# A graph network with two expert layers on one core: the mask of layer 1's hidden values moved from TensorE to VectorE

## The chip, the cores and the metric

The kernel runs on one core of a Trainium2 chip. The metric is the device time of one execution in microseconds (us). A core has five engines that run side by side and wait for one another through semaphores: TensorE (PE in the profile, with its weight loads shown apart as PEld), VectorE (DVE), ScalarE (ACT), GpSimd (POOL) and SyncE (SP). Each engine takes its instructions in a fixed order, which is settled when the program is built.

## The reference

`x` has 6250 rows (nodes) of 256 numbers; a list of 100,000 edges has a source, a target and a weight for each. There are two layers, and each has two parts, each added to `x`:

- a graph part: rows of a normalized `x` are gathered by edge source, scaled by the edge's weight and summed into the edge's target row, with a 256 x 256 weight before or after;
- a feed-forward part with experts: 8 experts mixed by a softmax in layer 0; in layer 1, 32 experts of which each token uses one.

The last part, cut to what matters here:

```python
logits = xf @ router_w.T + router_b
idx = jnp.argmax(logits, axis=-1)                       # one of 32 experts for each token
h = jnp.einsum('nd,ndh->nh', xf, jnp.take(W1, idx, axis=0)) + jnp.take(b1, idx, axis=0)
h = jax.nn.relu(h)                                      # 64 hidden values of that expert
out = jnp.einsum('nh,nhd->nd', h, jnp.take(W2, idx, axis=0)) + jnp.take(b2, idx, axis=0)
x = x + jax.nn.relu(out)
```

## The kernel before, in words

Nodes lie in 49 tiles of 128. An early stage sorts the edges, layer 0 follows, and from about 1700 us on layer 1 runs to the end. Only layer 1 matters here.

**The experts of layer 1.** All 32 experts' hidden values are computed for every token, 32 x 64 = 2048 of them, in NC1 = 16 chunks of 128 (two experts a chunk), with the hidden values on the partitions and the tokens along the free dimension. The values of experts not chosen have to become 0, so that the second product, which sums over all 2048, leaves the chosen expert's alone. The tokens go in blocks: one of three tiles and 23 of two (384 and 256 tokens). For each block:

- `norm_a` and `norm_b` normalize the tiles (`stats`, `scaled_tile`) and turn them with TensorE (`transposed`) into `nT`.
- `begin1` computes the logits (`pl`, L1227), finds the largest on VectorE (L1232 to L1238), and makes a one-hot of the chosen expert four times side by side (`hots`, ScalarE, L1240), turned by TensorE (`pg`, L1243) and copied to `hotT` (ScalarE, L1245): partition q has a 1 for the tokens whose expert is q modulo 32. VectorE also writes `cold`, its complement (L1247).
- `hidden1` makes chunk c: two products of W1 with `nT` into a PSUM tile `ph` (L1254; each is float32 and shows as two matmul instructions), then a product of `sel` with `cold` added to it (L1257, bfloat16). `sel` holds -2^127 where a hidden row belongs to the expert of that partition, so every hidden value of an expert not chosen gets a huge negative number added, and the relu on ScalarE (`hm`, L1259) makes it 0. `sel` is made once by VectorE (L1296).
- `outs1` multiplies `hm` with W2 and adds into the PSUM tile `py` (L1270); for the first chunk also the zeroing product L1264 and the chosen expert's bias (L1268). `end1` adds the relu of `py` to X (L1277) and writes the rows out.

**The graph sums of layer 1** run between these products. Of 782 columns of 128 edges, 64 are summed early and 718 in this stage. `columns1` takes for each column: a gather of 128 rows of `h1` by an indirect DMA issued from GpSimd (L215, 23 buffers `g`), a copy scaled by the weights on ScalarE (L245) and what that copy's rounding left on VectorE (L246), both into `m` (12 buffers), a one-hot `s` of the targets on VectorE for three columns at a time (L236, 5 buffers), and one product `acc` on TensorE (L293). Every eight columns a half tile of sums is complete: copied and added (L266 to L278), and after two of them turned and multiplied by the layer's weight (`by_weight`, L223 to L229) into X. The next block can begin when its tiles are there.

**The order.** The loop over blocks and chunks is written out: `sums.upto(...)` takes as many columns as a plan has set for that point, `hidden1` for the next chunk goes ahead of `outs1` for this one, and `begin1` of the next block stands in the middle of the present one (`rest`). A scheduler then settles each engine's order. In steady state a block of two tiles has 16 chunks and 32 columns. `ph` shares three PSUM buffers with `by_weight`, and `hm` has four.

Of the kernel before, what the change touches and what calls it, by code (L numbers as in the profile page):

```python
# [8 lines left out]
F32 = mybir.dt.float32  # L9
F32R = mybir.dt.float32r  # L10
BF = mybir.dt.bfloat16
# [41 lines left out]
def gnn_ffn_kernel(ctx: ExitStack, tc: tile.TileContext, a, out):  # L53
# [72 lines left out]
    good1 = const.tile([P, 1], F32, name="good1")  # L126
    off = const.tile([P, 1], F32, name="off")

    which_x = const.tile([P, NX1], F32, name="which_x")
    nc.gpsimd.iota(which_x, pattern=[[1, NX1]], base=0, channel_multiplier=-1, allow_small_or_imprecise_dtypes=True)  # L130
    order = const.tile([P, NX1], F32, name="order")
    nc.gpsimd.iota(order, pattern=[[-1, NX1]], base=NX1, channel_multiplier=0, allow_small_or_imprecise_dtypes=True)
    edges_rec, edges_val = a["edges_rec"], a["edges_val"]
# [697 lines left out]
    with outs_ctx, tc.tile_pool(name="layer0", bufs=1) as wp, \  # L831
# [367 lines left out]
        for t in blocks1[0]:  # L1199
            sT = wp.tile([P, 2, P], F32, tag="hT0", name="sT", bufs=2)  # L1200
            firsts.append(by_weight(psum, first_sums[:, t, :], sT, t, ("agg", 2) if t else ("tr", 1)))
            next(firsts[-1])
        for part in firsts:
            next(part)
        sums.upto(cum[-1] + NE + 1)
        add_missing(hs, (3, 4))
    sorted_ctx.close()
# [2 lines left out]
    with tc.tile_pool(name="layer1", bufs=1, reuse_waits="tile") as wp, \  # L1210
            tc.tile_pool(name="psum_y1", bufs=1, space=bass.MemoryType.PSUM, reuse_waits="tile") as psum_y:

        sel_x = wp.tile([P, NX1, H1], BF, name="sel")
        sel = sel_x.rearrange("q (c s) i -> q c (s i)", s=2)
        nought = wp.tile([P, 2 * D], BF, name="nought")

        done = []

        def begin1(pool, tiles, *ready):

            n = len(tiles)
            nw = n * P
            nT = norm_b(pool, psum, tiles, *ready)
            pl = psum.tile([P, NB, NX1], F32, tag="tr", name="pl", bufs=1)
            for j in range(n):
                for k in range(2):
                    nc.tensor.matmul(pl[:, j, :], nT[:, k, j * P:(j + 1) * P], rw[:, k, :],  # L1227
                                     start=(k == 0), stop=(k == 1))
            hot = work.tile([P, NB, NX1], F32, tag="hot", name="hot")
            top = work.tile([P, NB], F32, tag="top", name="top")  # L1230
            g, m = hot[:, :n, :], top[:, :n]
            nc.vector.tensor_tensor(g, pl[:, :n, :], br1[:, None, :].to_broadcast([P, n, NX1]), OP.add)  # L1232
            nc.vector.tensor_reduce(m, g, AX.X, OP.max)
            nc.vector.tensor_tensor(g, g, m[:, :, None].to_broadcast([P, n, NX1]), OP.is_equal)

            nc.vector.tensor_tensor(g, g, order[:, None, :].to_broadcast([P, n, NX1]), OP.mult)
            nc.vector.tensor_reduce(m, g, AX.X, OP.max)
            nc.vector.tensor_tensor(g, g, m[:, :, None].to_broadcast([P, n, NX1]), OP.is_equal)  # L1238
            hots = work.tile([P, NB, P // NX1, NX1], F32, tag="hots", name="hots", bufs=1)
            nc.scalar.activation(hots[:, :n], g[:, :, None, :].to_broadcast([P, n, P // NX1, NX1]), AF.Copy)  # L1240
            pg = psum.tile([P, NB * P], F32, tag="tr", name="pg", bufs=1)
            for j in range(n):
                turned = nc.tensor.transpose(pg[:, j * P:(j + 1) * P], hots[:, j], ident)  # L1243
            hotT = pool.tile([P, NB * P], BF, tag="hotT", name="hotT", bufs=2)
            done[:] = [turned, nc.scalar.activation(hotT[:, :nw], pg[:, :nw], AF.Copy)]  # L1245
            cold = pool.tile([P, NB * P], BF, tag="cold", name="cold", bufs=2)
            done.append(nc.vector.tensor_scalar(cold[:, :nw], pg[:, :nw], 0.5, None, op0=OP.is_lt))  # L1247
            return nT, hotT, cold, nw

        def hidden1(pool, block, c):  # L1250
            nT, _, cold, nw = block
            ph = psum.tile([P, NB * P], F32, tag="mm", name="ph", bufs=3)
            for k in range(2):
                nc.tensor.matmul(ph[:, :nw], w1f[:, k, c * P:(c + 1) * P], nT[:, k, :nw],  # L1254
                                 start=(k == 0), stop=False)

            nc.tensor.matmul(ph[:, :nw], sel[:, c, :], cold[:, :nw], start=False, stop=True)  # L1257
            hm = pool.tile([P, NB * P], F32, tag="hm", name="hm", bufs=4)
            nc.scalar.activation(hm[:, :nw], ph[:, :nw], AF.Relu, bias=b1[:, c:c + 1])  # L1259
            return hm  # L1260

        def outs1(block, c, now, py, n):
            for i in range(0, n, 2) if c == 0 else ():
                nc.tensor.matmul(py[:, i:i + 2, :], nought[:, :P], nought, start=True, stop=True)  # L1264
            for j in range(n):
                cols = slice(j * P, (j + 1) * P)
                if c == 0:
                    nc.tensor.matmul(py[:, j, :], block[1][:, cols], b2, start=False, stop=False,  # L1268
                                     skip_group_check=True)
                nc.tensor.matmul(py[:, j, :], now[:, cols], w2f[:, c, :], start=False, stop=(c == NC1 - 1),  # L1270
                                 skip_group_check=True)
# [12 lines left out]

        with tc.tile_pool(name="flow1", bufs=1, reuse_waits="tile") as flow:

            sums = Stream(columns1(flow, psum, range(NE, NREAL), h1, src_c, val_c, (5, EW + 6, 12, 4)))
            cum = [0] + [min(CS * (2 * tiles[-1] + 2) + CS // 2, NREAL) + LAG - NE for tiles in blocks1[1:]]
            rest = [(4, 2)] + [{2: (16, 6), 3: (12, 5), 4: (8, 3)}[len(tiles)] for tiles in blocks1[1:]]
            plans = aheads(cum, 2 * NC1, [r[0] for r in rest])  # L1290
            block = begin1(flow, *norm_a(blocks1[0]))

            behind = ExitStack()
            for ins in done:
                behind.enter_context(tc.issue_after(ins.ins))
            nc.vector.tensor_scalar(sel_x, which_x[:, :, None].to_broadcast([P, NX1, H1]), 0.0, FAR,  # L1296
                                    op0=OP.is_equal, op1=OP.mult)
            nc.vector.memset(nought, 0.0)
            hm = hidden1(flow, block, 0)
            for b, tiles in enumerate(blocks1):  # L1300
                n = len(tiles)
                last = b + 1 == len(blocks1)
                py = psum_y.tile([P, NB, D], F32, tag="y", name="py", bufs=1)
                mine = block
                for c in range(NC1):
                    sums.upto(plans[b][2 * c])
                    now = hm
                    if c + 1 < NC1:
                        hm = hidden1(flow, block, c + 1)
                    elif not last:  # L1310
                        block = after
                        hm = hidden1(flow, block, 0)
                    sums.upto(plans[b][2 * c + 1])
                    if b == 0 and c == 3:
                        behind.close()
                    outs1(mine, c, now, py, n)

                    if not last and c == NC1 - 1 - rest[b][0] // 2:
                        after = norm_a(blocks1[b + 1])
                    if not last and c == NC1 - 1 - rest[b][1]:  # L1320
                        after = begin1(flow, *after)
                end1(flow, tiles, py)

        with tc.tile_pool(name="slow1", bufs=1) as flow:

            def again():
                for t in range(NT):
                    block = begin1(flow, *norm_a([t]))
                    py = psum_y.tile([P, NB, D], F32, tag="y", name="py", bufs=1)
                    for c in range(NC1):  # L1330
                        outs1(block, c, hidden1(flow, block, c), py, 1)
                    end1(flow, [t], py)

            aggregate_any(psum, h1, True, again)
# [49 lines left out]
```

## Time and profile before

| | us |
|---|---|
| median of 3 runs | 2732.94 (2728.65 to 2740.33) |
| the profiled execution | 2729.55 |
| its span | 2727.7 |
| TensorE busy | 2589.7 (95%) |
| VectorE busy | 1993.3 (73%) |
| GpSimd busy | 1664.9 (61%) |
| ScalarE busy | 1652.4 (61%) |
| first and last gather of layer 1 start (718) | 1701.7 and 2637.5 |
| last output product ends, last output DMA issued | 2720.4, 2721.3 |

The span runs from the first to the last event of the profile. Busy times are unions of what the profiler recorded. The ends of matmuls are modelled, since they are pipelined: how long a matmul really occupies TensorE is read from the start of the next. A line such as `L246 DVE ... m<-g,val_c,m` names line, engine, operation, the tile written and the tiles read. In timelines the first column is the start, the second the duration, and the bracket at the end tells how long the engine had been idle and what ended it.

### The profile page before, as it was taken

The page shows a single profiled execution, that of the slowest core. Times are in us where ns is not written, and L with a number is a line of the kernel's source. Part 1 is how long each engine was busy: PE and PEld are TensorE (multiplying, and loading weights), DVE is VectorE, ACT ScalarE, POOL GpSimd, SP SyncE. Part 2 cuts the span into 40 slices and gives each one's busy share as a digit, 9 for nine tenths or more (in the row PEclk, how much of TensorE's full clock was granted, in tenths as well). Part 3 has the DMA queues.
Part 4 walks back from the last instruction along what each step waited for, and adds up shares of the span by engine and source line. Part 5 has one row for each costly group of instructions (what it writes and reads, how often), then busy time and mean ns, then how long its engine had stood idle before and what let it go on. Part 6 is the DMA issues. An engine that isn't in the chain of part 4 may idle for free.

```text
span 2727.7 us, 39992 instructions
## 1 busy us (share of the span) xinstructions
PE 2589.7 (95%) x11526; PEld 1880.3 (69%) x11527; DVE 1993.3 (73%) x5360; ACT 1652.4 (61%) x3915; POOL 1664.9 (61%) x1633
## 2 busy tenths in 40 slices
PE   5998788989899999999999999999999999999998
PEld 2666576867556666666666656678888888888887
DVE  8999887877687687787786657576666666666651
ACT  6999576655555555555555454466566666666652
POOL 0000757766776766766767445777777777777750
PEclk9999898999899999999999999999999999999999
DMA  6111433332332322332333233333333333333320
GB/s 203 55 47 55 152 109 113 106 111 82 102 94 86 106 90 81 107 88 83 105 90 93 70 93 110 95 111 105 110 111 106 110 110 106 111 109 106 111 79 10
DMA packets 132481, 267.36 MB, mean 98 GB/s; under 512 B 30564, under 2 KB 79800, under 8 KB 132248
## 3 DMA queue, kind: packets, MB, share of 16 engines
q0 software_dynamic: 77520, 211.78, 26.5%
q1 hardware_dynamic: 52568, 51.56, 5.9%
q8 instruction: 94, 1.54, 0.2%
q10 hardware_dynamic: 2160, 1.34, 0.2%
q14 instruction: 139, 1.14, 0.1%
HBM read 238.90 MB, written 25.67 MB: 97 GB/s over the span
## 4 chain that ended last, share of the span: by engine, by line
PE 74%; DVE 12%; DMA 5%; ACT 4%; issue 3%; POOL 1%; ACTq 0%; DVEq 0%; POOLq 0%; SPq 0%
PE ph L971 19%; PE ph L1254 12%; PE py L1270 12%; PE py L983 10%; PE acc L293 6%; PE acc L910 5%; DMA g<-h,idx 4%; PE put L614 2%; DVE m L246 2%; PE ph L1257 1%; PE ph L228 1%; DVE to L603 1%; PE ph L702 1%; ACT m L245 1%; POOL g L215 1%
## 5 line engine op out<-in xcount | busy, mean ns | idle before, releaser
L215 POOL DMA_INDIRECT g<-h,idx x822 | 860.4, 1047 | 386.8 <-DVE m L246 98.7
L215 POOL DMA_INDIRECT g<-h,src_c x718 | 715.6, 997 | 237.5 <-issue 94.5
L974 ACT ACTIVATE hT<-ph,shift,scale 128x512 f32<-128x512 f32 (+3 forms) x544 | 348.9, 654 | 298.4 <-PE ph L971 288.2
L245 ACT ACTIVATE m<-g,w 128x256 fp32r<-128x256 f32 x822 | 374.9, 500 | 217.5 <-PE acc L910 129.0
L246 DVE SCALAR_TENSOR_TENSOR m<-g,val_c,m 128x256 fp32r<-128x256 f32 x718 | 345.3, 483 | 205.0 <-ACT m L245 198.1
L245 ACT ACTIVATE m<-g,val_c 128x256 fp32r<-128x256 f32 x718 | 359.7, 504 | 125.6 <-PE acc L293 94.2
L1270 PE MATMUL py<-w,hm 128*128 128x256 f32 x1568 | 406.8, 379 | 1.3 <-ACT hm L1259 1.2
L1254 PE MATMUL ph<-nT,w 128*128 128x256 f32 (+1 forms) x1536 | 407.1, 385 | 0.0
L246 DVE SCALAR_TENSOR_TENSOR m<-g,w,m 128x256 fp32r<-128x256 f32 x822 | 370.3, 474 | 45.5 <-ACT m L245 44.4
L971 PE MATMUL ph<-nT,w 128*128 128x512 f32 (+3 forms) x1088 | 383.1, 482 | 19.2 <-ACT hT L974 18.9
L293 PE MATMUL acc<-m,s 128*128 128x512 f32 x782 | 398.9, 521 | 1.1 <-DVE m L246 1.0
L971 PE MATMUL ph<-hT,w 128*128 128x512 f32 (+3 forms) x1088 | 385.3, 481 | 6.5 <-ACT hT L974 6.4
L983 PE MATMUL py<-wo,hT 128*128 128x256 f32 x1568 | 383.1, 384 | 7.0 <-ACT hT L974 4.2
L910 PE MATMUL acc<-m,s 128*128 128x512 f32 x833 | 346.5, 501 | 17.2 <-DMA g<-h,idx 11.1
L983 PEld LDWEIGHTS py<-wo,hT 128*128 128x128 f32 x1568 | 291.8, 191 | 77.1 <-DVE X L985 18.0
L1259 ACT ACTIVATE hm<-ph,b 128x256 f32<-128x256 f32 (+1 forms) x384 | 183.4, 478 | 245.6 <-PE ph L1257 244.5
L1254 PEld LDWEIGHTS ph<-nT,w 128*128 128x128 f32 x1536 | 289.8, 191 | 47.3 <-issue 1.8
L1270 PEld LDWEIGHTS py<-w,hm 128*128 128x128 f32 x1568 | 287.1, 190 | 41.4 <-ACT hm L1259 2.4
L971 PEld LDWEIGHTS ph<-nT,w 128*128 128x128 f32 x1088 | 189.8, 193 | 145.8 <-issue 103.8
L971 PEld LDWEIGHTS ph<-hT,w 128*128 128x128 f32 x1088 | 194.6, 194 | 106.1 <-issue 74.0
L236 DVE TENSOR_TENSOR s<-col,dl 128x384 fp32r<-128x384 f32 (+1 forms) x294 | 155.7, 530 | 147.5 <-PE acc L910 147.1
L910 PEld LDWEIGHTS acc<-m,s 128*128 128x128 f32 x833 | 158.5, 193 | 102.8 <-DVE m L246 42.7
(301 smaller groups left out, 3175.2 us busy)
## 6 DMA issues: line engine op xcount, KB each, us to landing
g<-h,idx POOLq DMA_INDIRECT x822, 2.8
g<-h,src_c POOLq DMA_INDIRECT x718, 2.8
h<-hs SPq DMA_DIRECT2D x53, 128.0 KB, 1.7
own<-hs SPq DMA_DIRECT2D x49, 128.0 KB, 1.8
own<-own SPq DMA_DIRECT2D x49, 128.0 KB, 2.3
X<-in_x_dram SPq DMA_DIRECT2D x12, 512.0 KB, 8.3
out_dram<-o SPq DMA_DIRECT2D x22, 256.0 KB, 2.7
h<-hs SPq DMA_DIRECT2D x9, 512.0 KB, 3.1
```

Of the source, the lines that this page charges most:

```text
L215: nc.gpsimd.indirect_dma_start(out=g, out_offset=None, in_=h, in_offset=bass.IndirectOffsetOnAxis(ap=idx, axis=0))
L236: nc.vector.tensor_tensor(s[:, :n], col[:, None, :].to_broadcast([P, n, P]), dl[:, j:j + n, None].to_broadcast([P, n, P]), OP.is_equal)
L245: nc.scalar.activation(m[:, 0, :], g, AF.Copy, scale=w)
L246: newest[:] = [nc.vector.scalar_tensor_tensor(m[:, 1, :], g, w, m[:, 0, :], op0=OP.mult, op1=OP.subtract)]
L293: nc.tensor.matmul(acc, s[:, (j - js.start) % SJ, :], m, start=opens, stop=done)
L910: summed = nc.tensor.matmul(acc, s[:, j % SJ, :], m, start=(j == 0), stop=(j == EW - 1))
L971: nc.tensor.matmul(ph[:, :nw], (w1, w2)[layer][:, e, k, m * P:(m + 1) * P], src[:, k, :nw], start=(k == 0), stop=(k == 1))
L974: nc.scalar.activation(hT[:, m, :nw], ph[:, :nw], AF.Relu, bias=shift[:, layer, c:c + 1], scale=scale[:, layer, c:c + 1])
L983: nc.tensor.matmul(py, hT[:, k, j * P:(j + 1) * P], wo[:, e, k, :], start=(k == 0), stop=(k == 1))
L1254: nc.tensor.matmul(ph[:, :nw], w1f[:, k, c * P:(c + 1) * P], nT[:, k, :nw], start=(k == 0), stop=False)
L1259: nc.scalar.activation(hm[:, :nw], ph[:, :nw], AF.Relu, bias=b1[:, c:c + 1])
L1270: nc.tensor.matmul(py[:, j, :], now[:, cols], w2f[:, c, :], start=False, stop=(c == NC1 - 1), skip_group_check=True)
```

## The change

The mask goes from TensorE to VectorE. `sel`, `cold` and the product L1257 go. In their place:

- `begin1` makes one more product on TensorE after `hotT`: `ids`, a matrix whose row q holds the number q in all columns for q < 32 and 0 below, times `hotT` gives the number of the chosen expert of each token, on all partitions. ScalarE copies it to `chosen` (bfloat16).
- `expert`, made once, holds for each hidden row and chunk the number of the expert it belongs to.
- `hidden1` applies the relu as before, and then VectorE multiplies `hm` in place by 1 where `chosen` equals the row's `expert`, and by 0 elsewhere. Both tensor inputs of this instruction are in SBUF.
- The loop keeps two chunks of `hidden1` ahead of `outs1` instead of one, and in the first block the next block's `norm_a` and `begin1` come one chunk earlier.

```diff
-    which_x = const.tile([P, NX1], F32, name="which_x")
-    nc.gpsimd.iota(which_x, pattern=[[1, NX1]], base=0, channel_multiplier=-1, allow_small_or_imprecise_dtypes=True)
+    which_x = const.tile([P, NC1], F32, name="which_x")
+    nc.gpsimd.iota(which_x, pattern=[[2, NC1]], base=0, channel_multiplier=0, allow_small_or_imprecise_dtypes=True)
...
-            cold = pool.tile([P, NB * P], BF, tag="cold", name="cold", bufs=2)
-            done.append(nc.vector.tensor_scalar(cold[:, :nw], pg[:, :nw], 0.5, None, op0=OP.is_lt))
-            return nT, hotT, cold, nw
+            pe = psum.tile([P, NB * P], F32, tag="tr", name="pe", bufs=1)
+            nc.tensor.matmul(pe[:, :nw], ids, hotT[:, :nw], start=True, stop=True)
+            chosen = pool.tile([P, NB * P], BF, tag="chosen", name="chosen", bufs=2)
+            nc.scalar.activation(chosen[:, :nw], pe[:, :nw], AF.Copy)
+            return nT, hotT, chosen, nw
...
                 nc.tensor.matmul(ph[:, :nw], w1f[:, k, c * P:(c + 1) * P], nT[:, k, :nw],
-                                 start=(k == 0), stop=False)
-
-            nc.tensor.matmul(ph[:, :nw], sel[:, c, :], cold[:, :nw], start=False, stop=True)
+                                 start=(k == 0), stop=(k == 1))
             hm = pool.tile([P, NB * P], F32, tag="hm", name="hm", bufs=4)
             nc.scalar.activation(hm[:, :nw], ph[:, :nw], AF.Relu, bias=b1[:, c:c + 1])
+            nc.vector.scalar_tensor_tensor(hm[:, :nw], chosen[:, :nw], expert[:, c:c + 1], hm[:, :nw],
+                                           op0=OP.is_equal, op1=OP.mult)
...
-            rest = [(4, 2)] + [{2: (16, 6), 3: (12, 5), 4: (8, 3)}[len(tiles)] for tiles in blocks1[1:]]
+            rest = [(6, 3)] + [{2: (16, 6), 3: (12, 5), 4: (8, 3)}[len(tiles)] for tiles in blocks1[1:]]
...
+            nc.vector.scalar_tensor_tensor(expert, part.to_broadcast([P, NC1]), float(H1), which_x,
+                                           op0=OP.is_ge, op1=OP.add)
+            nc.vector.scalar_tensor_tensor(ids, part.to_broadcast([P, P]), float(NX1), part.to_broadcast([P, P]),
+                                           op0=OP.is_lt, op1=OP.mult)
...
-            nc.vector.tensor_scalar(sel_x, which_x[:, :, None].to_broadcast([P, NX1, H1]), 0.0, FAR,
-                                    op0=OP.is_equal, op1=OP.mult)
             nc.vector.memset(nought, 0.0)
-            hm = hidden1(flow, block, 0)
+            hms = [hidden1(flow, block, c) for c in range(2)]
...
-                    now = hm
-                    if c + 1 < NC1:
-                        hm = hidden1(flow, block, c + 1)
+                    now = hms.pop(0)
+                    if c + 2 < NC1:
+                        hms.append(hidden1(flow, block, c + 2))
                     elif not last:
-                        block = after
-                        hm = hidden1(flow, block, 0)
+                        hms.append(hidden1(flow, after, c + 2 - NC1))
```

More of the change, by code (lines that the diff above doesn't have):

```diff
@@ L1202, in gnn_ffn_kernel @@
             next(firsts[-1])
-        for part in firsts:
-            next(part)
+        for rest in firsts:
+            next(rest)
         sums.upto(cum[-1] + NE + 1)
@@ L1211, in gnn_ffn_kernel @@
             tc.tile_pool(name="psum_y1", bufs=1, space=bass.MemoryType.PSUM, reuse_waits="tile") as psum_y:
-        sel_x = wp.tile([P, NX1, H1], BF, name="sel")
-        sel = sel_x.rearrange("q (c s) i -> q c (s i)", s=2)
+        expert = wp.tile([P, NC1], F32, name="expert")
+        ids = wp.tile([P, P], BF, name="ids")
         nought = wp.tile([P, 2 * D], BF, name="nought")
@@ L1245, in begin1 @@
             done[:] = [turned, nc.scalar.activation(hotT[:, :nw], pg[:, :nw], AF.Copy)]
-            cold = pool.tile([P, NB * P], BF, tag="cold", name="cold", bufs=2)
-            done.append(nc.vector.tensor_scalar(cold[:, :nw], pg[:, :nw], 0.5, None, op0=OP.is_lt))
-            return nT, hotT, cold, nw
+            pe = psum.tile([P, NB * P], F32, tag="tr", name="pe", bufs=1)
[3 more added lines that the diff above has]
+            return nT, hotT, chosen, nw
         def hidden1(pool, block, c):
-            nT, _, cold, nw = block
+            nT, _, chosen, nw = block
             ph = psum.tile([P, NB * P], F32, tag="mm", name="ph", bufs=3)
@@ L1322, in gnn_ffn_kernel @@
                 end1(flow, tiles, py)
+                block = after
         with tc.tile_pool(name="slow1", bufs=1) as flow:
```

## The prediction

> **What bounds the kernel now.** The change lies wholly in layer 1, which fills the span from about 1700 us to its end at 2727.7 us, so I read the profile for that stage alone, starting with the busy times by stretch (us of the stretch, then TensorE, weight loads, VectorE, ScalarE, GpSimd, the granted clock, DMA share, GB/s):
>
> ```profile
> core 0: us, PE busy (x) PEld busy (x) DVE busy (x) ACT busy (x) POOL busy (x), PEclk, DMA share, GB/s
> 1720.00:1900.00 180.00, 175.51 (x820) 137.12 (x820) 121.77 (x301) 104.68 (x244) 138.40 (x136) 0.99 0.36 105
> 1900.00:2600.00 700.00, 698.79 (x3455) 572.89 (x3454) 481.83 (x1175) 426.79 (x996) 535.49 (x541) 1.00 0.37 109
> ```
>
> TensorE is busy 699 of 700 us at full clock, which alone would make it the bound. GpSimd looks idle a quarter of the time, and that is the trap. The view of waits shows what its idle time consists of (total, times, longest):
>
> ```profile
> ACT m L245 <- PE acc L293: 94.2, 223, 1.6
> POOL g L215 <- issue: 88.6, 291, 0.3
> POOL g L215 <- DVE m L246: 57.3, 188, 0.3
> ACT m L245 <- DMA g<-h,src_c: 18.6, 28, 1.6
> ```
>
> Between 1720 and 2720 us no pause of the gather queue is longer than 0.3 us, whatever it is put down to. Its timeline has 0.30 us in front of every gather, and a gather that nothing disturbs lasts 0.946 (the median of 718). So GpSimd runs without a break from 1701.7 to 2637.5 us: 718 gathers, one each 1.30 us, and it cannot issue faster than one in 1.246. TensorE needs 41.43 us for a block of two tiles (from one `pl` in the chain of waits to the next, 2560.65 to 2602.08) and takes in 32 columns, one each 1.295 us. **Two engines are full at nearly the same rate.** From column 180 on ScalarE's m waits for TensorE's acc (94 us) rather than for gathers (18.6 us, all but 0.9 of it before 1900): TensorE is the bound there, with no room behind it.
>
> Why gathers take 1.30 and not 1.246 is seen in the timeline (start, duration):
>
> ```profile
> 2315.24 0.56 DVE L236 TENSOR_TENSOR s<-col,dl_c 128x384 fp32r<-128x384 f32 x1
> 2315.28 1.33 POOL L215 DMA_INDIRECT g<-h,src_c  x1 [0.30 <-DVE hot L1238]
> ...
> 2323.20 0.42 DVE L267 TENSOR_TENSOR sums<-sums,acc 128x256 f32<-128x256 f32 x1 [0.78 <-ACT sums L266]
> 2323.20 0.95 POOL L215 DMA_INDIRECT g<-h,src_c  x1 [0.30 <-issue]
> ```
>
> In the first pair both inputs of the VectorE instruction are in SBUF, and the gather lasts 0.38 us too long; in the second one input is in PSUM and the gather is undisturbed. It holds for the stage: of the 541 gathers from 1900 to 2600 us, those that find VectorE idle 0.1 us after their start last 0.003 us longer than 0.946 on average (179 of them), those that find L267 0.004 (31), those that find m of L246, with two SBUF inputs, 0.071 (163), and s of L236 0.133 (86). A held gather goes on when that VectorE instruction ends.
>
> **The change part by part.** The rows it touches, from the groups by shape between 1720 and 2720 us (busy us, mean ns):
>
> ```profile
> L246 DVE SCALAR_TENSOR_TENSOR m<-g,val_c,m 128x256 fp32r<-128x256 f32 x718 | 345.3, 483 | 205.0 <-ACT m L245 198.1
> L236 DVE TENSOR_TENSOR s<-col,dl_c 128x384 fp32r<-128x384 f32 x240 | 134.4, 560 | 18.3 <-PE acc L293 14.5
> L1257 PE MATMUL ph<-cold,sel 128*128 128x256 bf16 x368 | 100.2, 273 | 0.0
> L1247 DVE TENSOR_SCALAR cold<-pg 128x256 bf16<-128x256 f32 x23 | 9.6, 418 | 2.9 <-ACT hotT L1245 2.9
> ```
>
> Removed on TensorE: 384 mask products. Their 273 ns is a modelled end; what one occupies is read from starts, at the end of the kernel where no gathers are left:
>
> ```profile
> 2710.12 1.03 PE L1254 MATMUL ph<-nT,w 128*128 128x256 f32 x4
> 2710.98 0.27 PE L1257 MATMUL ph<-cold,sel 128*128 128x256 bf16 x1
> 2711.09 1.03 PE L1270 MATMUL py<-w,hm 128*128 128x256 f32 x4
> ```
>
> From 2710.98 to 2711.09 is 0.108 us (mean over neighbours). 368 of these and 16 half as long again are 42.3 us. Added on TensorE: 24 products with `ids`, 2.6 us. If TensorE alone decided, the gain would be 40 us. ScalarE gains 24 copies of 0.38 us, at 61% load and off the path. VectorE loses `sel` (1.2 us), 24 `cold` (10 us), and gains 384 multiplies. The multiply (two SBUF inputs, one bf16, 256 columns) does not occur before; the nearest row is L246, same operation and width: 0.483 us. A PSUM-reading twin, L1277, takes 0.42 and 0.56 is the 384-wide s: bounds 0.42 and 0.56, 345 of them (those of the chunks before 2637.5 us) 145 to 193 us; I take 167. VectorE, 69% busy now, comes to about 83% of a stage of similar length: full enough to be late, not the bound.
>
> The wait added is hm on VectorE: the multiply waits for ScalarE's relu, and behind it stand m and s of later columns. The look-ahead becomes two chunks, so between a chunk's ph and its py TensorE has five acc and two chunks' worth of other products, about 4.5 us, against 0.47 for the relu plus 0.48 for the multiply and some queueing: covered; uncovered it would cost what it is late, some 0.5 us a chunk. In `begin1` the product with `ids` follows `pg` after two ph and one acc (about 0.65 us) and waits for `hotT`, which is ready 0.55 us after `pg` at 2315.87: no more than a few tenths a block. No DMA and no other queue is moved.
>
> With the TensorE share of a block down to 41.43 - 16 x 0.108 + 0.11 = 39.8 us, 1.244 a column, **GpSimd is late next**: its floor is 1.246. From there only the holding counts. Call e the mean extra time of a gather: now 0.997 - 0.946 = 0.051. Instructions with two SBUF inputs (m, s and 38 us of half-tile sums) fill 517 us of the 923 in which columns are processed, 56%; with 167 more it is 71% of some 960 us. What e becomes is not in the trace, and bounds are far apart:
> - low: 0, as the gathers from 1711 to 1718 us, spaced 1.25 beside an idle VectorE, or 0.02 if they happen to fall between instructions;
> - in proportion, 0.051 x 71/56 = 0.065;
> - in proportion from the stretch in which TensorE waits for gathers, 1720 to 1900 us, whose gathers last 138.40/136 = 1.018, e 0.072: 0.091. There m runs as soon as its gather lands, and what is queued behind it runs just when the next gather starts;
> - high: at random moments, 71% x half of 0.483 = 0.17.
>
> I take 0.091, since the changed stage is of that kind throughout: gather-bound. The last gather then starts at 2637.5 + 717 x 0.040 = 2666 us. Behind it lie 90.2 us now. 39 mask products go (4.2 us). About 5 us more go because TensorE trails less: now column 700 is summed 18.7 us after its gather starts, while in the changed instruction order the multiply of a chunk stands behind an m only 7 columns ahead of the chunk's py, 7 x 1.3 plus the shortest 3.5 us from gather to m, some 13 us. 2666 + 81 = 2747, plus the 1.85 us by which the profiled execution (2729.55) exceeds its span: **2749 us**. Those runs' median is 2732.94, 3.4 above that execution, so this is +0.7% of the one and +0.6% of the other. In general the time is 2749 + 717 x (e - 0.091).
>
> The Trainium skill has a rule that speaks against this change: "SBUF — State Buffer", section "Who interferes with whom", says that a VectorE instruction with two SBUF inputs and a GpSimd instruction that reads SBUF exclude each other, the later one fully blocked until the first is done. The rows at 2315 and 2323 us agree, but the page gives no price; taken literally for gathers at random moments it is the high end, 2806, where the mean extra of the rows gives 2730 to 2749.
>
> **The rivals.**
> - *The holding grows only in proportion* (e 0.065): 2730. For it: the 0.071 per meeting with an m, which would add only about 0.012 for 17% more of such meetings. Against it: the gather-bound stretch. No change to be seen; 0.25.
> - *The gathers slip between the multiplies* (e about 0.02): one place, GpSimd's start of a gather. A gather held until an instruction's end is back at the same point 1.246 us later; queued instructions start 0.40 us apart (three m in 1.26 us at 1720.36), 0.45 to 0.5 behind an s, so m, multiply and s take about 1.3, and the hold repeats with only some 0.05 us, and with none where VectorE is between columns. Time 2698; faster as soon as e is under 0.045, the bound of 0.5%. TensorE's 39.8 us a block does not let it go far below 2684. Against it: three without an s take 1.20, and the gather then meets the next at its start. 0.20.
> - *The gathers meet VectorE at random* (e 0.14 to 0.17): 2784 to 2806, taken as 2795. For it: from 1718 to 1726 us, with VectorE's instructions back to back, gathers last 1.67, 1.07, 1.36, 1.35, 0.99. Against: 179 of 541 still find it idle. 0.18.
> - *VectorE itself becomes the bound*: needs a multiply over 0.48 + (960 - 800)/345 = 0.94 us; no row comes near. That the change does not do what it says is excluded by the instruction order: no sel product is left.
>
> **How the numbers follow.** Forecast 0.37, the others as given. The measurement tells about 0.5%, 14 us. Faster is the slipping case, 0.20; within 0.5% (2716 to 2743, e 0.045 to 0.083) is the proportional case, 0.25; slower the forecast and the random case, 0.55. The range leaves out half of the random case and the best of the slipping one: 2700 to 2795; around the forecast alone 2743 to 2775.
>
> **What would show it.** Right: gathers' mean duration rises from 0.997 to about 1.04 with pauses still 0.3, the last starts near 2666, TensorE shows idle time in front of acc or py, waits of ScalarE's m for gathers outweigh those for acc, and 0.108 us a chunk is saved after the last gather. Wrong: TensorE still without gaps and a block near 39.8 us (the holding did not grow), or a multiply far from 0.48 us, or VectorE without gaps.

## The result, and the profile after

The changed kernel takes 2748.31 us (median of 9 runs, 2742.48 to 2753.94), the kernel before on the same chip 2732.18 (9 runs, 2728.29 to 2740.33): ratio 1.0057, 95% interval 1.0041 to 1.0072, slower by some 16 us. The profiled execution took 2752.75 us, with a span of 2750.9. It lies 4.4 us above its kernel's median, and the profiled execution of the kernel before 2.6 below its own, so the two profiles differ by 23.2 us where the medians differ by 16.

Busy times by stretch, of the kernel after (us of the stretch, then TensorE, weight loads, VectorE, ScalarE, GpSimd, granted clock, DMA share, GB/s):

```profile
core 0: us, PE busy (x) PEld busy (x) DVE busy (x) ACT busy (x) POOL busy (x), PEclk, DMA share, GB/s
1720.00:1900.00 180.00, 168.69 (x733) 134.19 (x732) 137.03 (x338) 105.58 (x244) 139.12 (x135) 0.96 0.35 104
1900.00:2600.00 700.00, 668.98 (x3126) 558.60 (x3125) 544.75 (x1390) 417.30 (x988) 540.38 (x524) 0.98 0.36 105
```

TensorE is no longer full: 669 of 700 us, where it was 699. VectorE went from 482 to 545 us. GpSimd has as much busy time as before (540 against 535 us) but starts 524 gathers in it instead of 541: each is longer.

Seven rows of the waits of the kernel after between 1720 and 2740 us (total, times, longest):

```profile
ACT m L245 <- DMA g<-h,src_c: 159.3, 243, 2.1
DVE hm L1260 <- ACT hm L1259: 74.1, 116, 1.9
ACT m L245 <- PE acc L293: 66.5, 75, 3.3
POOL g L215 <- issue: 64.6, 212, 0.3
POOL g L215 <- DVE m L246: 51.8, 170, 0.3
PEld tr L356 <- ACT nT L357: 32.3, 21, 4.1
POOL g L215 <- DVE hm L1260: 31.4, 103, 0.3
```

Two rows have changed places: ScalarE's m now waits 159 us for gathers (18.6 before) and 67 us for acc (94 before). The gathers' own pauses are still 0.3 us at the longest: the queue is full as before, and now everything else waits for it.

Three groups of the page of the kernel after (busy us, mean ns of one, idle time before them):

```profile
L215 POOL DMA_INDIRECT g<-h,src_c x718 | 740.4, 1031 | 242.8 <-issue 66.7
L246 DVE SCALAR_TENSOR_TENSOR m<-g,val_c,m 128x256 fp32r<-128x256 f32 x718 | 343.3, 480 | 157.0 <-ACT m L245 152.5
L1260 DVE SCALAR_TENSOR_TENSOR hm<-chosen,expert,hm 128x256 f32<-128x256 bf16 (+1 forms) x384 | 186.6, 486 | 77.4 <-ACT hm L1259 75.3
```

The mean gather went from 0.997 to 1.031 us. One held gather in the timeline of the kernel after (start, duration):

```profile
2035.10 0.48 DVE L246 SCALAR_TENSOR_TENSOR m<-g,val_c,m 128x256 fp32r<-128x256 f32 x1
...
2035.27 1.60 POOL L215 DMA_INDIRECT g<-h,src_c  x1 [0.30 <-DVE hm L1260]
...
2035.50 0.55 DVE L236 TENSOR_TENSOR s<-col,dl_c 128x384 fp32r<-128x384 f32 x1
```

It meets an m, and an s directly behind it; it ends at 2036.87, 0.82 us after the s does (2036.05). So a hold can run on through a second instruction that follows without a gap. It does so seldom, and behind an m more often than elsewhere: of 77 gathers held over 0.05 us by an m with an s directly behind it, 19 were held to the end of the s; of 74 held by a multiply with an m behind it, 1 to the end of the m; of 59 held by an s with an m behind it, 1 (before, after and e7_idle_sbuf together, 1720 to 2630 us).

The whole difference of the two spans lies in three terms, read from the starts of the first and last gather. The last two columns are experiments told below:

| us | before | after | e7_idle_sbuf | e12_psum_pad |
|---|---|---|---|---|
| first gather starts | 1701.7 | 1708.9 | 1697.0 | 1701.8 |
| from it to the last one's start (717 intervals) | 935.8 | 958.0 | 961.1 | 943.8 |
| from there to the span's end | 90.2 | 84.0 | 88.9 | 83.5 |
| span | 2727.7 | 2750.9 | 2747.1 | 2729.1 |
| mean of 718 gathers | 0.997 | 1.031 | 1.036 | 1.006 |

The kernel after loses 7.2 us at the first gather and 22.2 in the gathers' pace, and gains 6.2 behind the last one: 23.2 us of span. Part of the first loss is made up at once, since the kernel before has one long pause in its queue, in front of the second gather; its line in the timeline of before:

```profile
1705.71 0.94 POOL L215 DMA_INDIRECT g<-h,src_c  x1 [3.08 <-issue]
```

e12_psum_pad has one there too (4.19 us), the kernel after and e7_idle_sbuf have none. Counted from the second gather on, the kernel after starts 4.5 us late (1710.2 against 1705.7), and its pace costs 24.9 us more (956.7 against 931.8).

The gathers between 1900 and 2600 us, sorted by what VectorE does 0.1 us after they start: how many, and by how much they exceed 0.946 us in sum.

| VectorE | before | after | e7_idle_sbuf | e12_psum_pad |
|---|---|---|---|---|
| idle | 179, 0.3 | 91, 0.2 | 107, 0.3 | 108, 0.1 |
| m (L246) | 163, 11.3 | 188, 22.6 | 141, 15.3 | 160, 15.2 |
| s (L236) | 86, 11.4 | 75, 12.7 | 73, 13.1 | 80, 12.9 |
| the multiply | none | 88, 6.6 | 100, 12.1 | 101, 0.2 |
| all | 541, 24.8 | 524, 45.5 | 525, 44.1 | 535, 31.9 |

In these four traces 701 gathers of this stretch last over 0.05 us longer than 0.946, and every one of them ends 0.81 to 0.83 us after the end of a VectorE instruction that reads only SBUF: m, s, the multiply from SBUF, a half-tile sum or another with two tiles there, and in 16 cases `xn` (L362), which reads one tile and two numbers per row. None ends so after an instruction with an input in PSUM.

### The profile page after: what moved, and what is told of

The parts are those of the page before. It is cut to its first block, busy times and chain, and to the rows that moved or that the text cites. A ratio compares the mean times of both kernels' runs of the same rounds, so it can differ in the third digit from the quotient of the medians.

```text
span 2750.9 us, 39554 instructions
## 1 busy us (share of the span) xinstructions
PE 2574.7 (94%) x11167; PEld 1886.4 (69%) x11167; DVE 2115.4 (77%) x5721; ACT 1658.5 (60%) x3939; POOL 1690.1 (61%) x1633
## 4 chain that ended last, share of the span: by engine, by line
PE 59%; DVE 15%; DMA 13%; ACT 5%; issue 5%; POOL 2%; ACTq 0%; DVEq 0%; POOLq 0%; SPq 0%
PE ph L971 19%; PE py L983 10%; DMA g<-h,src_c 8%; PE py L1272 7%; PE ph L1256 7%; PE acc L910 5%; DMA g<-h,idx 4%; PE acc L293 3%; DVE m L246 3%; ACT m L245 2%; PE put L614 2%; POOL g L215 2%; DVE to L603 1%; PE ph L702 1%; PE pl L1227 1%
## 5 line engine op out<-in xcount | busy, mean ns | idle before, releaser
L215 POOL DMA_INDIRECT g<-h,src_c x718 | 740.4, 1031 | 242.8 <-issue 66.7
L246 DVE SCALAR_TENSOR_TENSOR m<-g,val_c,m 128x256 fp32r<-128x256 f32 x718 | 343.3, 480 | 157.0 <-ACT m L245 152.5
L293 PE MATMUL acc<-m,s 128*128 128x512 f32 x782 | 440.4, 576 | 1.1 <-DVE m L246 1.0
L1256 PE MATMUL ph<-nT,w 128*128 128x256 f32 (+1 forms) x1536 | 416.6, 390 | 0.0
L1272 PE MATMUL py<-w,hm 128*128 128x256 f32 x1568 | 414.6, 386 | 0.0
L246 DVE SCALAR_TENSOR_TENSOR m<-g,w,m 128x256 fp32r<-128x256 f32 x822 | 370.1, 474 | 41.7 <-ACT m L245 40.3
L910 PE MATMUL acc<-m,s 128*128 128x512 f32 x833 | 346.5, 501 | 15.1 <-DMA rw<-in_router_t_dram 11.0
L236 DVE TENSOR_TENSOR s<-col,dl 128x384 fp32r<-128x384 f32 (+1 forms) x294 | 155.5, 529 | 150.3 <-PE acc L910 150.1
L1260 DVE SCALAR_TENSOR_TENSOR hm<-chosen,expert,hm 128x256 f32<-128x256 bf16 (+1 forms) x384 | 186.6, 486 | 77.4 <-ACT hm L1259 75.3
```

Source lines behind the costliest of these rows:

```text
L215: nc.gpsimd.indirect_dma_start(out=g, out_offset=None, in_=h, in_offset=bass.IndirectOffsetOnAxis(ap=idx, axis=0))
L246: newest[:] = [nc.vector.scalar_tensor_tensor(m[:, 1, :], g, w, m[:, 0, :], op0=OP.mult, op1=OP.subtract)]
L293: nc.tensor.matmul(acc, s[:, (j - js.start) % SJ, :], m, start=opens, stop=done)
L910: summed = nc.tensor.matmul(acc, s[:, j % SJ, :], m, start=(j == 0), stop=(j == EW - 1))
L1260: nc.vector.scalar_tensor_tensor(hm[:, :nw], chosen[:, :nw], expert[:, c:c + 1], hm[:, :nw], op0=OP.is_equal, op1=OP.mult)
```

## The experiments

My theory was that GpSimd's queue of gathers sets the time, that it can run no faster than one in 1.246 us, and that a VectorE instruction with two inputs in SBUF holds a gather, so that what TensorE saves counts for little and the multiply costs what it holds. The rivals: the time VectorE is busy, or the changed order, did it; or TensorE alone sets the time.

e1 to e6 and e8 to e11 ran on chips on which the kernel before itself takes 3162 to 3204 us, with pauses of several us on every engine from about 200 us on, so their times are compared only with the kernel before on the same chip, and the microseconds expected for them were not to be met there. Waits of e8_psum between 2000 and 2900 us show it (total, times, longest):

```profile
POOL g L215 <- DVE m L246: 135.8, 135, 4.0
ACT m L245 <- issue: 105.9, 68, 7.1
POOL g L215 <- issue: 105.9, 298, 1.9
```

The queue of gathers has pauses of up to 4 us there, and is not full. How long one gather lasts, and what holds it, can be read on these chips all the same. e7 and e12 ran on chips that are like that of the main result, with one execution each beside one of the kernel before.

**e7_idle_sbuf: the multiply alone, TensorE's work left as it was.** The kernel before, with one more instruction behind the relu:

```diff
             nc.scalar.activation(hm[:, :nw], ph[:, :nw], AF.Relu, bias=b1[:, c:c + 1])
+            spare = pool.tile([P, NB * P], F32, tag="spare", name="spare", bufs=2)
+            nc.vector.scalar_tensor_tensor(spare[:, :nw], cold[:, :nw], good1, hm[:, :nw],
+                                           op0=OP.is_equal, op1=OP.mult)
```

> The kernel before, mask product kept, with one more VectorE instruction per chunk in layer 1: the multiply of the change, on the chunk's relu output in SBUF, into a tile that nobody reads. TensorE's work and what is computed stay those of before. My theory (a VectorE instruction with two SBUF inputs that runs 0.1 us after a gather's start holds that gather): the mean gather rises from 0.997 us to 1.02 to 1.05, and where gathers follow one another after 0.30 us the time rises by 718 times that rise, 17 to 38 us, ratio 1.006 to 1.014. Rival (the loss came from the order of the work, the wait on the relu or the smaller tiles, not from the instruction itself): mean gather 0.99 to 1.00 and ratio 1.000 to 1.002.

Measured: 2748.97 us against 2733.10 of the kernel before, ratio 1.0058 (one run each, so no interval); the 15.9 us are just under the bound of 17. The first gather starts 4.7 us earlier than in the kernel before, which was not expected and whose cause was not tested; without it the bound would have been met. The mean gather is 1.036 us. Busy time of e7_idle_sbuf by stretch, columns as above:

```profile
1900.00:2600.00 700.00, 686.95 (x3351) 562.30 (x3351) 548.68 (x1400) 410.15 (x963) 540.06 (x526) 0.99 0.36 106
```

Nobody reads what this instruction writes, no order around it was changed, and the mask product is still there; yet the gathers slow down as in the changed kernel. By the table of terms, e7's pace is only 3.2 us slower than that of the kernel after, and its end only 4.9 us longer: **beside this multiply, TensorE's 40 us are worth about 8 us.** That is one execution of each kernel, and nine executions of the kernel after lie up to 11 us apart; it is far from 40 all the same. The rival of the order is not needed: the multiply alone slows the gathers as much. The timeline of e7_idle_sbuf shows the hold and its condition (two pairs, start and duration):

```profile
1975.97 0.48 DVE L1261 SCALAR_TENSOR_TENSOR spare<-cold,good,hm 128x256 f32<-128x256 bf16 x1
1976.12 1.15 POOL L215 DMA_INDIRECT g<-h,src_c  x1 [0.30 <-DVE m L246]
...
2100.44 0.94 POOL L215 DMA_INDIRECT g<-h,src_c  x1 [0.30 <-DVE st L345]
2100.45 0.45 DVE L1261 SCALAR_TENSOR_TENSOR spare<-cold,good,hm 128x256 f32<-128x256 bf16 x1
```

In the first pair the multiply starts 0.15 us ahead of the gather, which then ends 0.82 us after the multiply. In the second the gather starts first, by 0.01 us, and nothing happens to it.

**e12_psum_pad: the same multiply, its second input in PSUM.** The changed kernel; relu written back into PSUM, and an unused tile that puts the gather buffers where they lay before:

```diff
+        spare = wp.tile([P, NX1 * H1 - P - 2 * NC1], BF, name="spare")
...
+            nc.vector.memset(spare[:, :2], 0.0)
...
-            nc.scalar.activation(hm[:, :nw], ph[:, :nw], AF.Relu, bias=b1[:, c:c + 1])
-            nc.vector.scalar_tensor_tensor(hm[:, :nw], chosen[:, :nw], expert[:, c:c + 1], hm[:, :nw],
+            nc.scalar.activation(ph[:, :nw], ph[:, :nw], AF.Relu, bias=b1[:, c:c + 1])
+            nc.vector.scalar_tensor_tensor(hm[:, :nw], chosen[:, :nw], expert[:, c:c + 1], ph[:, :nw],
                                            op0=OP.is_equal, op1=OP.mult)
```

> The kernel of e6_psum_pad: relu written back into PSUM and read there by the multiply, and the gather buffers where they lay before. Where gathers follow one another after 0.30 us, as in e7_idle_sbuf, my theory gives a mean gather of 0.985 to 1.005, so 1.285 to 1.305 per gather; a first gather at 1698 to 1703; a last one 717 times that later, at 2619 to 2639; and a tail of 79 to 86 us: a span of 2700 to 2723 and a time of 2702 to 2725, under the kernel before because the products that are gone shorten the tail. Rival 1 (the multiply costs its time wherever its input lies): mean gather 1.03, time 2738 to 2748. Rival 2 (TensorE is the only full engine once the gathers are not held): 2690 to 2698. That the late first gather comes from the order of the work would show as a first gather near 1709.

Measured: 2730.91 us against 2738.25 of the kernel before (one run each). That is under all nine runs of the kernel after and within the nine of the kernel before (2728.29 to 2740.33): the loss is gone, a gain is not shown. Busy time by stretch, the multiply's group and a pair of the timeline of e12_psum_pad, a fence for each:

```profile
1900.00:2600.00 700.00, 677.69 (x3182) 568.95 (x3181) 554.40 (x1412) 422.13 (x1004) 537.01 (x536) 0.99 0.38 108
```

```profile
L1261 DVE SCALAR_TENSOR_TENSOR hm<-chosen,expert,ph 128x256 f32<-128x256 bf16 (+1 forms) x384 | 184.4, 481 | 72.3 <-ACT ph L1260 69.7
```

```profile
2000.98 0.47 DVE L1261 SCALAR_TENSOR_TENSOR hm<-chosen,expert,ph 128x256 f32<-128x256 bf16 x1
...
2001.12 0.94 POOL L215 DMA_INDIRECT g<-h,src_c  x1 [0.30 <-DVE s L236]
```

VectorE is busier than in the kernel after (554 us against 545), the multiplies are as many and take nearly the same time (481 ns against 486; those of 256 columns 475 against 481), yet a gather that starts 0.14 us behind one is not held. So it is not VectorE's busy time (rival 1: 2738 to 2748). Nor does the time fall to 2690 to 2698, as it should if TensorE alone set it (rival 2). My own 2702 to 2725 was missed by 6 us: first gather (1701.8) and end (83.5) came as expected, the pace did not (1.316 us an interval, against at most 1.305). Of the 8 us that this makes, 4 are the pause in front of the second gather. By the second table the multiply holds nothing any more (0.2 us), but m and s hold 5.4 us more in these 700 us than in the kernel before; why they meet more gathers is open.

All meetings with a multiply between 1900 and 2600 us (on the pausing chips 2000 to 2900), by how far ahead of the gather it starts:

| multiply reads | kernels | 0.08 to 0.30 us ahead | 0.03 ahead to 0.08 behind |
|---|---|---|---|
| two inputs in SBUF | after, e7 | 98 gathers, +0.167 us, 94 held | 60, +0.005, none held |
| one in SBUF, one in PSUM | e12 | 43, +0.001, none held | 37, +0.002, none held |
| one in SBUF, one in PSUM | e8, e10, e11 | 116, +0.001, none held | 113, +0.003, none held |

Held means over 0.05 us longer than 0.946. The Trainium skill, "SBUF — State Buffer", section "Who interferes with whom", states both halves: leaving aside what it calls the 2-port modes, a VectorE instruction with at most one SBUF input does not contend with GpSimd, and one with two SBUF inputs contends with a GpSimd instruction that reads SBUF. It adds that the order of issue decides who blocks. The runs agree where VectorE comes first, and add the price. That a gather which comes first blocks VectorE they do not show: in the kernel before, m takes 0.483 us when it begins 0.05 to 0.45 us into a gather (198 of them), and 0.483 us when it begins 0.45 to 0.9 us into one (193).

At the border the order alone does not settle it. In e3_pad and e4_kept, told below, whose multiply reads SBUF on a pausing chip, 8 of 78 gathers of the last column are held, by up to 1.2 us: in all eight the multiply starts 0.01 to 0.02 us ahead, directly behind an m that still runs.

**e1_psum, e8_psum: relu back into PSUM, nothing else.** The two changed lines of e12, without the unused tile, on two chips.

> Only the operand of the multiply changes: ScalarE writes the relu back into PSUM in place, and VectorE multiplies from there, so the multiply has one input in SBUF instead of two; same number of VectorE instructions, same waits. Theory (GpSimd's gathers set the pace, and VectorE instructions with two SBUF inputs hold them): the mean gather falls from 1.031 us to 0.99 to 1.00, the last gather starts near 2638 us, and the time is 2715 to 2730 us, faster than before by a little. Rival (VectorE's load, or the wait of the multiply for the relu, delays the chunks): gathers may change but the time stays at 2740 to 2750.

> The changed kernel with layer 1's relu written back into its PSUM tile and the multiply reading that tile from PSUM: one SBUF input (chosen) and one PSUM input instead of two in SBUF; the multiply's count and size as in the change. On this chip GpSimd is expected to keep its 0.30 us between gathers. My theory: the mean gather falls from 1.031 us to 0.985 to 1.005 and the last gather starts at 2632 to 2650 (first one still late, near 1709), so the time is 2713 to 2732, ratio to the kernel before 0.993 to 1.000. Rival 1 (any VectorE instruction holds a gather in proportion to VectorE's busy time): mean gather 1.03, time 2745 to 2752. Rival 2 (TensorE's order sets the time): TensorE's work is that of the change, so 2745 to 2752 too, with a mean gather anywhere.

Measured: ratios 0.9999 (0.9967 to 1.0031) and 0.9999 (0.9971 to 1.0027); mean gather 0.991 and 0.999 us. The gathers come as expected: they last as long as without any multiply (0.990 to 0.998, next paragraph), where the same multiply from SBUF makes it 1.023 and 1.034 (e3_pad, e4_kept). The small gain in time that was expected does not show; the times say nothing of a full queue there.

**e2_nomask, e5_nomask2, e9_nomask: no mask at all in layer 1**, one kernel on three chips:

```diff
-            nc.vector.scalar_tensor_tensor(hm[:, :nw], chosen[:, :nw], expert[:, c:c + 1], hm[:, :nw],
-                                           op0=OP.is_equal, op1=OP.mult)
```

> The multiply is left out, so the values of experts not chosen are not made 0; TensorE is without the mask product, all else as in the changed kernel. Theory (gathers set the pace once TensorE is relieved): the mean gather is 0.99 to 1.02 us and the time 2718 to 2735 us, though TensorE has 40 us less work than before. Rival (TensorE was the only bound before, and what was lost is VectorE's time): about 2692 us.

> The kernel without the multiply once more (the values of experts not chosen are not made 0), since on the chip of the first four runs every engine paused for 1 to 5 us at a time and the kernel before took 3196 us. On a chip without these pauses: theory (gathers set the pace once TensorE is relieved): mean gather 0.99 to 1.02 us, time 2718 to 2735 us. Rival (TensorE was the only bound before): about 2692 us.

> The changed kernel with the multiply left out as well, so that no mask is applied in layer 1 and the output is not the reference's: TensorE's 40 us are saved and VectorE's 177 us are not added. My theory (the gathers are a queue that is full): the mean gather is 0.985 to 1.005, the pauses stay 0.30 us, and 718 gathers from 1709 end near 2632 to 2645; with a tail of 79 to 84 us the time is 2711 to 2729, so most of TensorE's 40 us is still not seen. Rival (TensorE was the only full engine): the time falls by all of it, to 2690 to 2696.

Measured: ratios 0.9937 (0.9912 to 0.9963), 0.9938 (0.9909 to 0.9966) and 0.9968 (0.9944 to 0.9991), 10 to 20 us by the ratios and 15 to 27 by the medians; mean gather 0.990, 0.998, 0.992. Even with no multiply at all, TensorE's 40 us are not seen in full (at most 29 by the intervals). As the queue is not full on these chips, this does not show that the gathers are what keeps the rest.

**e3_pad: the change with the unused tile alone** (its two lines in the diff of e12).

> The changed kernel with an unused tile of the size by which its fixed tiles became smaller (3.8 KB a partition), so that the gather buffers lie where they lay before. If the place of the buffers made the first gather wait for ScalarE's last reading of layer 0's sums (1708.9 instead of 1701.7 us), it starts near 1702 again, all gathers move by 7 us, and the time falls from 2748 to about 2741. If the late start has another cause or is made up for later: 2748.

Measured: ratio 0.9919 (0.9890 to 0.9948), so on this chip the change with the unused tile is 0.8% faster than the kernel before; mean gather 1.023 us, the multiplies met holding 0.127 each (93 of them). The first gather is what this run tells. Its line in the timeline of e3_pad, then that of the kernel after:

```profile
1939.01 0.94 POOL L215 DMA_INDIRECT g<-h,src_c  x1 [16.30 <-DVE m L246]
```

```profile
1708.95 0.94 POOL L215 DMA_INDIRECT g<-h,src_c  x1 [24.34 <-ACT first_sums L266]
```

In all seven runs with the change's smaller fixed tiles (after, e1, e2, e4, e5, e8, e9) this wait is 21.9 to 24.3 us and ends with ScalarE's `first_sums`; in the four with the unused tile, e12 among them, and in the kernel before it is 16.3 to 18.0 and ends with an m. It is a matter of place: the gather buffers came to lie where another tile was still in use. By the second gather 4.5 of the 7.2 us are left, as said above.

**e4_kept: the change, with a product of zeros on TensorE in the old product's place.**

```diff
-                                 start=(k == 0), stop=(k == 1))
+                                 start=(k == 0), stop=False)
+            nc.tensor.matmul(ph[:, :nw], nought[:, :P], chosen[:, :nw], start=False, stop=True)
```

> The changed kernel with a product as long as the removed mask product put back on TensorE in each chunk (zeros times the expert numbers, which adds nothing): VectorE as in the changed kernel, TensorE as before. Theory (TensorE is no longer the bound while gathers run): only the 39 products behind the last gather cost, 4 us, and at most a few more where TensorE was short of room: 2752 to 2760 us. Rival (TensorE's work still counts throughout): 2787 us.

Measured: ratio 1.0027 (0.9999 to 1.0055), mean gather 1.034 us. The unmodified change did not run on this chip; against e3_pad there, which differs by the unused tile too, it is 1.1% longer (33 us by the medians). That is nearer to the rival's 39 us than to the expected 4 to 12: on this chip, where the queue is not full, TensorE's work does count.

**e6_psum_pad, e11_psum_pad: the kernel of e12 on two pausing chips.**

> Both edits that the theory asks for: the relu goes back into PSUM, so that the multiply has one input in SBUF, and the spare tile keeps the gather buffers where they lay before. On a chip where the kernel before takes 2732 us, theory (gathers set the pace, held by VectorE instructions with two SBUF inputs, and started late because of the buffers' place): mean gather 0.99 to 1.00 us, first gather near 1702 us, last near 2632 us, time 2708 to 2722 us, faster than both kernels. Rival (VectorE's load or the added wait decides): 2735 to 2750 us.

> e8_psum with an unused tile in the fixed pool, of the size by which the change had made the fixed tiles smaller (3.8 KB per partition), so that the gather buffers lie where they lay in the kernel before. My theory: the first gather starts at 1700 to 1703 instead of near 1709, and the time is 5 to 9 us below that of e8_psum: 2706 to 2725, the fastest of all that compute the reference. Rival (the late first gather comes from the order of the work, not from the place): first gather still near 1709 and the time that of e8_psum within 2 us.

Measured: ratios 0.9980 (0.9957 to 1.0003) and 0.9985 (0.9959 to 1.0011); mean gather 0.990 and 0.995 us. A gain over the kernel before, and e11 over e8 on the same chip (0.9999), lies within the intervals. The wait before the first gather ends as in the kernel before, as expected.

**e10_idle_psum: the idle multiply of e7, on PSUM.** As e7, with `ph[:, :nw]` in the place of `hm[:, :nw]`.

> The kernel before, mask product kept, with one more VectorE instruction per chunk in layer 1 into a tile that nobody reads, as in e7_idle_sbuf, but on the chunk's masked product in PSUM instead of its relu output in SBUF. My theory: one SBUF input does not hold a gather, so the mean gather stays at 0.99 to 1.005 and the time at 2730 to 2738, against 2749 with the SBUF input. Rival (VectorE's busy time or the place of the instruction did it): mean gather 1.02 or more and 2745 to 2752.

Measured: ratio 1.0053 (1.0032 to 1.0074), mean gather 0.996 us. The gathers are not held, as expected; the time rises all the same, which my theory does not say. On these chips added work on VectorE (here 17 us) and on TensorE (e4) costs time though the queue is not full, and e3_pad (0.9919) even stands ahead of e1_psum (0.9999), on the same chip, though its gathers are the longer ones. What sets the time there stays open. One candidate was not tried: with the relu in PSUM, `ph` is freed only after the multiply. Nor did e7 and e10, which differ by the operand alone, run on chips of one kind.

## Why the prediction was right

- **Two full engines, GpSimd late next.** Right. TensorE's load fell to 669 of 700 us, the pauses stayed 0.3 (that GpSimd ran without a break from 1701.7 us overlooks the 3.08 us at 1705.7), and a block takes 42.9 us (from one `pl` in the chain of waits to the next, 2157.84 to 2629.21 for 11 blocks), where TensorE's own work was put at 39.8. e7, which keeps that work, runs at the same pace.
- **The holding by instructions with two SBUF inputs.** Right, and shown: the SBUF and the PSUM form of one instruction, nearly equal in time and equal in number, hold 94 of 98 and none of 43.
- **e goes to 0.091.** Measured 1.031 - 0.946 = 0.085, so 4 us too much; proportional growth (0.065), slipping (0.02) and chance (0.14 to 0.17) were all further off. The reason given was half the story: it named what is queued behind m. In the kernel after only 6.6 of the 20.7 us more lie with gathers that meet the multiply; 11.3 lie with m, of which 8.4 where an s follows the m at once (35 such meetings before, 2.8 us in sum; 51 after, 11.2). The multiply pushes m and s together in part: about half of this growth lies with ten meetings (4.7 us) in which it runs directly ahead of the m, and nearly all of the rest with eight in which the output addition L1279 does. Why these came to meet gathers is open.
- **The last gather at 2666.** It started at 2666.9, by errors that cancel: the pace cost 22 us instead of 29 (4 of these 7 us are e, 3 the pause in the kernel before), and 7 us came from the late first gather, which I did not foresee. So it is luck that the forecast of 2749 meets the median of 2748.31 within 1 us: its terms missed by 3 to 7 us, and the nine executions lie up to 11 us apart. I had looked at what instructions the change removes, not at where tiles come to lie when fixed ones shrink by 3.8 KB per partition.
- **The multiply.** 0.481 us for 256 columns, against 0.483. VectorE at 78% of the stretch instead of 83%: back to back, an instruction starts 0.08 us before the one ahead ends in the records (2035.10 + 0.48 and 2035.50 above), and these overlaps grew from 37 to 72 us of the 700.
- **What was costed at nothing.** hm's wait for VectorE: among TensorE's waits between 1720 and 2740 us there is none of `py` for the multiply. The product with `ids` waits 5.7 us in 22 blocks, 0.26 each.
- **The end, 81 us.** 84.0. The products that went save 0.108 us a chunk: the chunk period falls from 1.835 to 1.726. But TensorE trails less by 2.2 us, not 5: the last column is summed 21.9 us after its gather starts, 24.0 before.
- **What would show it.** TensorE's idle time is not ahead of acc or py but at `tr` (L356), 32 us of weight loads waiting for the copies nT, which mostly stand on ScalarE behind an m that waits for its gather; ahead of `py` there are 3.9 us, for the output addition of the block before (L1279). The records of acc became longer (583 ns in the median, 481 before, 1900 to 2600 us), but that is not lateness: it depends on the product ahead. Already in the kernel before acc lasts 0.58 us behind the float32 `py` and 0.48 behind the mask product, which the kernel after lacks. e7, whose gathers are as late but which keeps that product, has 482 ns, and e12 582. From the timeline of before:

```profile
2322.05 0.27 PE L1257 MATMUL ph<-cold,sel 128*128 128x256 bf16 x1
2322.08 0.48 PE L293 MATMUL acc<-m,s 128*128 128x512 f32 x1
...
2322.39 1.03 PE L1270 MATMUL py<-w,hm 128*128 128x256 f32 x4
...
2323.07 0.58 PE L293 MATMUL acc<-m,s 128*128 128x512 f32 x1
```

## What to carry to other kernels

Look at an engine's pauses before its busy share: GpSimd, busy for 76% of the stretch, had no pause but the 0.30 us in front of each gather, and was full. Before work is moved to VectorE, look what runs on GpSimd beside it and count the inputs that lie in SBUF. Here the same multiply, with nearly the same duration, cost 14 us of pace more from SBUF than from PSUM, or 18 counted from the second gather on (one execution each). And where tiles shrink, see what the buffers behind them come to overlap.

## What the runs showed of the hardware

- Who is first decides, except at the border: a multiply with two SBUF inputs that starts 0.08 to 0.30 us ahead of a gather holds it (94 of 98); one that starts 0.03 us ahead of the gather's start to 0.08 behind it does not (none of 60 in the kernel after and e7; 8 of 78 in e3_pad and e4_kept), though both then run side by side for 0.4 us.
- A held gather ends 0.82 us after the VectorE instruction, for all 701 that were held in four traces; where two of them follow each other, seldom after the second (2035.27 us, 1.60 long).
- On some chips the same kernel takes 16 to 17% longer (3162 to 3204 us against 2732), from pauses of the engines and not from longer instructions: the gathers last 0.99 to 1.03 us there too, and m on VectorE takes 0.480 us on average in e8_psum as in the kernel after. Why the engines pause there is not known.
